# Spectral layer on one core: an inverse transform from quarter-length even waves, one pool of shared buffers, stores from another queue

## The chip, the core and the metric

The kernel runs on one NeuronCore of a Trainium2 chip (trn2). Its engines are TensorE (PE in the profile, its weight loads PEld), VectorE (DVE), ScalarE (ACT), GpSimd (POOL) and SyncE (SP), which only issues transfers. A transfer (DMA) can be issued from the queue of SyncE, ScalarE or GpSimd; an issue waits in its queue behind everything ahead of it. The metric is the device time of one execution in microseconds; the time given for a kernel is the median of its runs. All arithmetic is in float32; a float32 matmul shows as two records in the profile.

## The reference, cut to what matters

The input has shape (4, 512, 128, 64): batch, time, node n, channel c. Layer 0 (a recurrent mixing, two convolutions and a feed-forward part, with layer norms) takes most of the time and the change doesn't touch it. Layer 1 is:

```python
def layer1(x, w_real, w_imag):                 # x: (B=4, T=512, N=128, C=64)
    trend = moving_average(x, 25)              # over time, edges repeated
    seasonal = x - trend
    xs = rfft(seasonal, axis=1)[:, :128]       # the first 128 modes
    ys = einsum('bmnc,cmk->bknc', xs, w_real + 1j * w_imag)   # mixes modes, per channel
    filt = irfft(pad(ys), n=512, axis=1)       # modes above 127 are zero
    return trend + filt
```

## The kernel before

Layer 0 leaves its result in four arrays of HBM, `x4[b]`, each 512 times by 8192 columns (node and channel). Layer 1 (`layer1` in the source) works on them in slabs of 512 columns: 16 slabs per batch, each loaded as a tile `xin` of 128 partitions by 4 blocks of 128 times by 512 columns, 1024 KB, from SyncE's queue (`slab`, L763). It handles the batches in two pairs, and each pair goes through three stages.

*Transform* (32 slabs of a pair). VectorE forms sums and differences of the two halves of the time axis (L780, tiles `uv`). TensorE multiplies the sums with the waves of the even modes and the differences with those of the odd modes (L791), into PSUM banks of the tag `a`, on top of a correction for the edges of the moving average (L787), whose 12 first and 12 last times come from GpSimd's queue as four small transfers per slab (`edge`, L775 and L776, two buffers). ScalarE copies the result into the spectrum `xf` (L796), which holds two planes, real and imaginary, for both batches of the pair. The modes lie in an order of their own on the partitions, `MODES`: before, the 64 even ones and then the 64 odd ones.

*Mix*. In 16 groups of four channels, the weights are loaded (`w`, L803, 512 KB from SyncE's queue, two buffers); GpSimd writes their negated imaginary part beside them (L804); TensorE multiplies spectrum and weights (L811, L815) into banks of the tag `b`, and VectorE and ScalarE copy back into `xf`.

*Inverse* (`invert`, 16 slabs for each batch of the pair). `waves(s)` makes the filtered signal of slab `s`. For each of the two quarters `i` of the first half of the time axis it multiplies real and imaginary plane, even modes (partitions 0 to 63) and odd modes (64 to 127) apart, so eight matmuls with 64 rows (L840), into four banks `a`. ScalarE copies the even part out (L845), and VectorE forms even plus odd, the signal of the quarter, and even minus odd, that of the same quarter of the second half (L848, tiles `pm`). `trends(s)` loads the slab once more, and six small pieces of 12 times each (`halo`, L859 and L862, SyncE's queue, two buffers), computes the moving average of each of the four blocks (L865, and L868 for what reaches over from the neighbouring blocks) into four banks `b`, adds the filtered signal in place (L871), and stores the slab (L872, from ScalarE's queue).

The slabs of transform and inverse share three buffers. The order of TensorE's work is the order of the source (`manual_schedule`): waves 0, waves 1, trends 0, waves 2, trends 1 and so on, so that the last two `trends` of a batch have no waves between them. For the other engines a scheduler fixes the order of the instructions when the kernel is built; each queue then works strictly in that order, and a tile is reused when everything that reads it is done.

Of the kernel before, what the change touches and what calls it, by code (L numbers as in the profile page):

```python
# [10 lines left out]
F32 = mybir.dt.float32  # L11
AF = mybir.ActivationFunctionType
ALU = mybir.AluOpType
# [3 lines left out]
P = 128  # L17
# [14 lines left out]

MODES = np.concatenate([np.arange(0, M, 2), np.arange(1, M, 2)])
EPS = 1e-5
# [5 lines left out]
@with_exitstack  # L40
def conv_seq_kernel(
    ctx: ExitStack,
    tc: tile.TileContext,
    x: bass.AP,
    xt: bass.AP,
    vecs: bass.AP,
    wkvr: bass.AP,
    wo: bass.AP,
    wdec: bass.AP,
    wconv: bass.AP,  # L50
    fbias: bass.AP,
    w1: bass.AP,
    fb1: bass.AP,
    w2: bass.AP,
    fb2: bass.AP,
    wri: bass.AP,
    dft: bass.AP,
    dfte: bass.AP,
    idft: bass.AP,
    avg: bass.AP,  # L60
    avgh: bass.AP,
    out: bass.AP,
):
    B = x.shape[0]
    dram = ctx.enter_context(tc.tile_pool(name="dram", bufs=1, space=DRAM))
    x4 = [dram.tile([T, D], F32, tag=f"x4_{b}", name=f"x4_{b}") for b in range(B)]

    layer0(tc, dram, x, xt, vecs, wkvr, wo, wdec, wconv, fbias, w1, fb1, w2, fb2, x4)
    layer1(tc, x4, wri, dft, dfte, idft, avg, avgh, out)

# [648 lines left out]
@with_exitstack  # L719
def layer1(ctx, tc, x4, wri, dft, dfte, idft, avg, avgh, out):  # L720

# [18 lines left out]
    dfte_sb = load("dfte_sb", dfte)  # L740
    idft_sb = load("idft_sb", idft)
    avg_sb = load("avg_sb", avg)
    avgh_sb = load("avgh_sb", avgh)

    def bank(tag):
        return ps.tile([P, SL], F32, tag=tag, name=tag)
# [14 lines left out]
    def slab(b, s):  # L761
        xin = io.tile([P, NT, SL], F32, tag="xin", name="xin", bufs=3)
        nc.sync.dma_start(  # L763
            xin, x4[b][:, s * SL : (s + 1) * SL].rearrange("(c p) d -> p c d", p=P)
        )
        return xin

    def transform(b, xf):

        for s in range(NS):  # L770
            c = slice(s * SL, (s + 1) * SL)
            xin = slab(b, s)
            edge = io.tile([H, SL], F32, tag="edge", name="edge")
            for r in range(2):
# [23 lines left out]
    def mix(xf):  # L798

        xc = xf.rearrange("p b r (a c l) -> p b r a c l", c=H, l=2)  # L800
        for g in range(H // CG):
            w = io.tile([P, CG, 3, M], F32, tag="w", name="w")
            nc.sync.dma_start(w[:, :, 0:2, :], wri[:, g * CG : (g + 1) * CG, :, :])  # L803
            nc.gpsimd.tensor_scalar(w[:, :, 2, :], w[:, :, 1, :], -1.0, 0.0, ALU.mult, ALU.add)  # L804
            for q in range(CG // 2):
                c0 = g * CG + 2 * q
                py = [bank("b"), bank("b")]
                for r in range(2):
                    for j in range(2):
                        o = py[r][:, j * G * NF : (j + 1) * G * NF]  # L810
                        nc.tensor.matmul(  # L811
                            o, lhsT=w[:, 2 * q + j, r, :], rhs=xc[:, :, 0, :, c0 + j, :], start=True,
                            stop=False,
                        )
                        nc.tensor.matmul(  # L815
                            o, lhsT=w[:, 2 * q + j, 2 if r == 0 else 0, :], rhs=xc[:, :, 1, :, c0 + j, :],
                            start=False, stop=True,
# [9 lines left out]
    def invert(b, xf):  # L827
# [3 lines left out]
        def waves(s):  # L831

            c = slice(s * SL, (s + 1) * SL)
            out = []
            for i in range(2):
                eo = [bank("a"), bank("a")]
                for r in range(2):
                    for h in range(2):
                        hs = slice(h * H, (h + 1) * H)
                        nc.tensor.matmul(  # L840
                            eo[h], lhsT=idft_sb[hs, r, i, :], rhs=xf[hs, r, c],
                            start=(r == 0), stop=(r == 1),
                        )
                even = io.tile([P, SL], F32, tag="even", name="even")
                nc.scalar.copy(even, eo[0])  # L845
                pm = io.tile([P, 2, SL], F32, tag=f"uv{i}", name="pm")
                for k, op in enumerate((ALU.add, ALU.subtract)):
                    nc.vector.tensor_tensor(pm[:, k, :], even, eo[1], op)  # L848
                out.append(pm)
            halves[s] = out  # L850

        def trends(s):
            c = slice(s * SL, (s + 1) * SL)
            xin = slab(b, s)
            halo = io.tile([P, SL], F32, tag="halo", name="halo")
            for j in range(NT):
# [13 lines left out]
            for j in range(NT):  # L870
                nc.vector.tensor_tensor(by_n(xin[:, j, :]), by_n(po[j]), by_c(pm[j % 2][:, j // 2, :]), ALU.add)  # L871
            nc.scalar.dma_start(out[b, :, c].rearrange("(c p) d -> p c d", p=P), xin)  # L872

# [16 lines left out]
def _constants():  # L890
# [20 lines left out]
    idft = waves * weight  # L911
    idft[1, k == 0] = 0.0
    tiles = [slice(i * P, (i + 1) * P) for i in range(NT)]
    avg = np.stack([a[s, s].T for s in tiles], axis=1)
    avgh = np.zeros((NT, 32, P))
    for j, s in enumerate(tiles):
# [5 lines left out]
        "dfte": dfte.reshape(2 * 32, M),  # L922
        "idft": idft[:, :, : T // 2].reshape(2, M, 2, P).transpose(1, 0, 2, 3),
        "avg": avg,
# [5 lines left out]
def _inputs(x, i):  # L930
# [13 lines left out]
    for a in range(2):  # L944
        for b in range(2):
            wconv[a * H : (a + 1) * H, b * H : (b + 1) * H] = taps[a - b + 1]
    wconv[H:, 2 * H :] = taps[0]
    wconv[:H, 2 * H :] = taps[2]
    b = x.shape[0]
    a = {  # L950
# [11 lines left out]
        "fb2": np.concatenate([i["ffn_b2"]] * 2)[:, None],  # L962
        "wri": np.stack([i["w_real"], i["w_imag"]], axis=2)[:, MODES][..., MODES].transpose(1, 0, 2, 3),
        **_constants(),
# [19 lines left out]
```

## Time and profile before

The time is 4107.79 us (median of 3 runs, 4098.11 to 4113.56); the profiled run has a span of 4116.7 us. Layer 1 takes about the last 1130 us of it:

| stage | from to (us) | length | PE busy | DVE busy | ACT busy | DMA GB/s |
|---|---|---|---|---|---|---|
| transform, first pair | 2988 to 3147 | 159 | 158.1 | 73.8 | 39.9 | 249 |
| mix | 3147 to 3259 | 112 | 111.8 | 26.8 | 23.7 | 71 |
| inverse | 3259 to 3553 | 294 | 275.8 | 159.5 | 36.6 | 235 |
| transform, second pair | 3553 to 3706 | 153 | 153.0 | 75.7 | 39.9 | 262 |
| mix | 3706 to 3817 | 111 | 110.8 | 26.4 | 23.7 | 67 |
| inverse | 3817 to 4108 | 291 | 273.2 | 157.5 | 36.6 | 232 |

How to read a group of instructions in the profile: source line, engine and operation; what is written and read by the program's names; shapes; number of instructions; after the bar the time in which at least one of them ran and the mean nanoseconds of one; after the second bar the idle time of the engine just ahead of them, and what ended most of it. Matmuls overlap, so the mean of one is longer than the distance from one start to the next; the prediction works with distances. In a timeline a row is a start, a length and the instructions that were merged into it, with the wait ahead of it in brackets.

### The profile page before, as it was taken

The numbers are of one execution on the slowest core, as the hardware profiler recorded it, in microseconds if no ns is written. First come the engines' busy times: TensorE is split into PE (matmuls) and PEld (weight loads), VectorE is DVE, ScalarE is ACT, GpSimd is POOL, SyncE is SP. The second block draws the span as 40 slices with busy tenths as digits, with TensorE's granted clock in tenths as the row PEclk, the third lists the DMA queues.
The fourth block names the chain that finished last, engine by engine and source line by source line (L and its number), as shares of the span: only waits on it lengthen the run. The fifth ranks groups of instructions, "written<-read, shape, count | busy, mean of one in ns | idle before, by whom it ended". The sixth has DMA issues, their size and how long they took to land. (4 is left out here: it accounts for less than half of the span.)

```text
span 4116.7 us, 46561 instructions
## 1 busy us (share of the span) xinstructions
PE 3908.1 (95%) x16939; PEld 1460.7 (35%) x16939; DVE 2493.7 (61%) x3168; ACT 1796.8 (44%) x2396; POOL 527.2 (13%) x942
## 2 busy tenths in 40 slices
PE   9999989999999999999999888999899999999998
PEld 4433322233333223333322322333325733228433
DVE  1145549975556997555699899655443355542555
ACT  2112336545555554555565678777622211122111
POOL 0000012310000221000122122000032000130000
PEclk9989999999999999999999999999999999999999
DMA  5466647776664776666477676555385377882577
GB/s 170 157 209 235 208 132 250 252 246 228 238 224 152 240 258 237 222 234 231 157 249 250 217 251 238 187 168 184 133 254 168 95 258 243 272 245 72 186 241 239
DMA packets 445854, 867.80 MB, mean 211 GB/s; under 512 B 35321, under 2 KB 101561, under 8 KB 445625
## 3 DMA queue, kind: packets, MB, share of 16 engines
q1 hardware_dynamic: 347136, 588.34, 44.6%
q0 software_dynamic: 62464, 207.66, 14.4%
q10 hardware_dynamic: 36024, 68.82, 4.5%
q8 instruction: 135, 2.21, 0.2%
q14 instruction: 95, 0.77, 0.1%
HBM read 596.18 MB, written 268.50 MB: 210 GB/s over the span
## 5 line engine op out<-in xcount | busy, mean ns | idle before, releaser
L616 PE MATMUL pa<-mid,w_sb 128*64 128x512 f32 x2048 | 499.7, 609 | 43.0 <-DVE x4t L621 42.6
L609 ACT ACTIVATE mid<-m,fb_sb 128x1024 f32<-128x1024 f32 x256 | 285.0, 1113 | 303.4 <-PE m L605 303.0
L621 DVE SCALAR_TENSOR_TENSOR x4t<-pa,fb_sb,x 128x512 f32<-128x512 f32 x252 | 188.0, 746 | 263.2 <-PE pa L616 263.2
L605 PE MATMUL m<-x,w_sb 64*128 64x512 f32 x1008 | 290.8, 650 | 5.7 <-ACT mid L609 5.2
L555 DVE SCALAR_TENSOR_TENSOR to<-xh,vec,to 128x512 f32<-128x512 f32 x384 | 277.0, 744 | 12.6 <-issue 8.6
L609 ACT ACTIVATE mid<-c,fb_sb 128x1024 f32<-128x1024 f32 x256 | 283.3, 1107 | 1.4 <-PE c L605 1.2
L845 ACT COPY even<-a 128x512 f32<-128x512 f32 x128 | 71.7, 588 | 480.3 <-PE b L865 145.8
L865 PE MATMUL b<-xin,avg_sb 128*128 128x512 f32 x512 | 246.6, 626 | 35.5 <-DMA xin<-x 32.4
L605 PE MATMUL c<-x,w_sb 64*128 64x512 f32 x1008 | 264.5, 598 | 0.7 <-ACT mid L609 0.7
L616 PEld LDWEIGHTS pa<-mid,w_sb 128*64 128x64 f32 x2048 | 124.8, 136 | 387.7 <-issue 229.8
L780 DVE TENSOR_TENSOR uv<-xin 128x1024 f32<-128x1024 f32 x128 | 151.2, 1222 | 172.4 <-PE a L791 135.7
L327 PE MATMUL a<-xp,both 128*128 128x512 f32 x512 | 247.5, 610 | 6.4 <-DVE both L324 5.9
L848 DVE TENSOR_TENSOR pm<-even,a 128x512 f32<-128x512 f32 x256 | 159.3, 683 | 143.5 <-ACT even L845 109.7
L791 PE MATMUL a<-uv,dft_sb 128*64 128x512 f32 x1024 | 241.2, 612 | 0.0
L840 PE MATMUL a<-xf,idft_sb 64*128 64x512 f32 x1024 | 239.8, 602 | 0.6 <-DVE pm L848 0.4
L871 DVE TENSOR_TENSOR xin<-b,pm 128x512 f32<-128x512 f32 x256 | 159.1, 684 | 116.4 <-PE b L868 116.4
L634 ACT COPY ob<-pt 128x512 f32<-128x512 f32 x256 | 148.9, 582 | 165.5 <-PE pt L630 165.2
L324 DVE TENSOR_SCALAR both<-both,vec 128x192 f32<-128x192 f32 x192 | 53.2, 316 | 251.9 <-DMA both<-in_wkvr 220.6
L796 ACT COPY xf<-a 128x512 f32<-128x512 f32 x128 | 80.9, 632 | 266.1 <-PE a L791 266.1
L215 PE MATMUL st<-x,ones 128*32 128x512 f32 x512 | 182.4, 615 | 14.3 <-DVE x L491 14.3
L582 ACT ACTIVATE kd<-kd,vec 128x512 f32<-128x512 f32 x256 | 193.5, 809 | 4.3 <-DVE kd L574 4.2
L494 ACT ACTIVATE sq<-x 128x1024 f32<-128x1024 f32 x128 | 134.6, 1052 | 117.7 <-DVE x L491 117.4
(234 smaller groups left out, 6879.3 us busy)
## 6 DMA issues: line engine op xcount, KB each, us to landing
xp<-in_xt SPq DMA_DIRECT2D x256, 512.0 KB
xin<-x SPq DMA_DIRECT2D x128, 1024.0 KB
kx<-x SPq DMA_DIRECT2D x224, 512.0 KB
x<-x POOLq DMA_DIRECT2D x128, 512.0 KB, 4.2
kh<-to SPq DMA_DIRECT2D x128, 512.0 KB
x<-ob POOLq DMA_DIRECT2D x64, 1024.0 KB, 6.6
out<-xin ACTq DMA_DIRECT2D x64, 1024.0 KB
both<-in_x SPq DMA_DIRECT2D x96, 512.0 KB
```

Of the source, the lines that this page charges most:

```text
L215: nc.tensor.matmul(st[32 * q : 32 * q + 32, :], lhsT=ones, rhs=src[:, j, :], start=first, stop=last,)
L327: nc.tensor.matmul(pa[:, k, :], lhsT=wq[:, j, k * P : (k + 1) * P], rhs=xp[:, j, :], start=first and j == 0, stop=last and j == 1,)
L555: nc.vector.scalar_tensor_tensor(to[:, j, :], xh[:, j, k : SL + k], vec[:, w, c], to[:, j, :], ALU.mult, ALU.add)
L582: tc.keep_in_program_order(nc.scalar.activation(d[:, j, :], d[:, j, :], AF.Identity, bias=vec[:, B4, c], scale=vec[:, G4, c]))
L605: nc.tensor.matmul(pm[:, h, :], lhsT=w1_sb[hs, m * P : (m + 1) * P], rhs=x3[hs, :], start=True, stop=True)
L609: nc.scalar.activation(mid, pm, AF.Gelu_apprx_tanh, bias=fb1_sb[:, m : m + 1])
L616: nc.tensor.matmul(pa[h * H : (h + 1) * H, :], lhsT=w2_sb[:, m, :], rhs=mid[:, h, :], start=(m == 0), stop=(m == 1),)
L621: nc.vector.scalar_tensor_tensor(x4t, pa, fb2_sb, x3s[c // 2][:, c % 2, :], ALU.add, ALU.add)
L791: nc.tensor.matmul(pf[r][h * H : (h + 1) * H, :], lhsT=dft_sb[:, h, i, r, :], rhs=uv[h][:, i, :], start=False, stop=(i == 1),)
L840: nc.tensor.matmul(eo[h], lhsT=idft_sb[hs, r, i, :], rhs=xf[hs, r, c], start=(r == 0), stop=(r == 1),)
L848: nc.vector.tensor_tensor(pm[:, k, :], even, eo[1], op)
L865: nc.tensor.matmul(po[j], lhsT=avg_sb[:, j, :], rhs=xin[:, j, :], start=True, stop=False)
```

## The change

The even modes are split by parity once more, which halves the work on them: multiples of 4 are the same in the first and second quarter of the time axis, and the modes 2, 6, 10 and so on change sign. So one matmul each over a quarter of the axis is enough for them, and VectorE forms sum and difference (`even`) before it adds and subtracts the odd part (`pm`) as before. For this the spectrum is laid out anew by the mix: plane 0 holds the even modes, real and imaginary parts of the multiples of 4 on partitions 0 to 63 and those of the others on 64 to 127, and plane 1 all odd modes, real parts and imaginary parts. A matmul of the inverse thus sums over real and imaginary part at once. The weights come from the host in this layout, and GpSimd makes their second plane in four operations (swapped parts, with a sign on one of them).

Further: slabs and weights share one pool of five buffers of 8 KB per partition, instead of three for slabs and two for weights; `halo` and `edge` share two; and the finished slab is stored from GpSimd's queue instead of ScalarE's. The matrices `idft` are replaced by `idfte` (128 by 128) and `idfto` (128 by 2 by 128).

```diff
-MODES = np.concatenate([np.arange(0, M, 2), np.arange(1, M, 2)])
+MODES = np.concatenate([np.arange(0, M, 4), np.arange(2, M, 4), np.arange(1, M, 2)])
...
-        xin = io.tile([P, NT, SL], F32, tag="xin", name="xin", bufs=3)
+        xin = io.tile([P, NT, SL], F32, tag="big", name="xin", bufs=5)
...
-            edge = io.tile([H, SL], F32, tag="edge", name="edge")
+            edge = io.tile([P, SL], F32, tag="edge", name="edge")
...
-            w = io.tile([P, CG, 3, M], F32, tag="w", name="w")
-            nc.sync.dma_start(w[:, :, 0:2, :], wri[:, g * CG : (g + 1) * CG, :, :])
-            nc.gpsimd.tensor_scalar(w[:, :, 2, :], w[:, :, 1, :], -1.0, 0.0, ALU.mult, ALU.add)
+            w = io.tile([P, CG, 2, 2, M], F32, tag="big", name="w", bufs=5)
+            nc.sync.dma_start(w[:, :, 0, :, :], wri[:, g * CG : (g + 1) * CG, :, :])
+            for r, n in ((0, 2), (1, 1)):
+                wr, wi = (w[:, :, k, r, :].rearrange("p c (n i m) -> p c n i m", n=n, i=2) for k in range(2))
+                for i, sign in ((0, -1.0), (1, 1.0)):
+                    if n == 1:
+                        src, dst = wr[:, :, 0, 1 - i, :], wi[:, :, 0, i, :]
+                    else:
+                        src, dst = wr[:, :, :, 1 - i, :], wi[:, :, :, i, :]
+                    nc.gpsimd.tensor_scalar(dst, src, sign, 0.0, ALU.mult, ALU.add)
...
-            out = []
+            ev, od = [bank("a"), bank("a")], [bank("a"), bank("a")]
+            for h in range(2):
+                hs = slice(h * H, (h + 1) * H)
+                nc.tensor.matmul(ev[h], lhsT=idfte_sb[hs, :], rhs=xf[hs, 0, c], start=True, stop=True)
             for i in range(2):
-                eo = [bank("a"), bank("a")]
-                for r in range(2):
-                    for h in range(2):
-                        hs = slice(h * H, (h + 1) * H)
-                        nc.tensor.matmul(
-                            eo[h], lhsT=idft_sb[hs, r, i, :], rhs=xf[hs, r, c],
-                            start=(r == 0), stop=(r == 1),
-                        )
-                even = io.tile([P, SL], F32, tag="even", name="even")
-                nc.scalar.copy(even, eo[0])
+                nc.tensor.matmul(od[i], lhsT=idfto_sb[:, i, :], rhs=xf[:, 1, c], start=True, stop=True)
+            even = io.tile([P, 2, SL], F32, tag="ev", name="even")
+            two = io.tile([P, SL], F32, tag="even", name="two")
+            nc.scalar.copy(two, ev[1])
+            halves[s] = []
+            for i, op in enumerate((ALU.add, ALU.subtract)):
+                nc.vector.tensor_tensor(even[:, i, :], ev[0], two, op)
+            for i in range(2):
                 pm = io.tile([P, 2, SL], F32, tag=f"uv{i}", name="pm")
                 for k, op in enumerate((ALU.add, ALU.subtract)):
-                    nc.vector.tensor_tensor(pm[:, k, :], even, eo[1], op)
-                out.append(pm)
-            halves[s] = out
+                    nc.vector.tensor_tensor(pm[:, k, :], even[:, i, :], od[i], op)
+                halves[s].append(pm)
...
-            halo = io.tile([P, SL], F32, tag="halo", name="halo")
+            halo = io.tile([P, SL], F32, tag="edge", name="halo")
...
-            nc.scalar.dma_start(out[b, :, c].rearrange("(c p) d -> p c d", p=P), xin)
+            nc.gpsimd.dma_start(out[b, :, c].rearrange("(c p) d -> p c d", p=P), xin)
```

## The prediction

> **What bounds the kernel now.** I read the page first (busy shares, slices, costliest groups), then a table of stages, then the timeline of a few slabs, then who waited for whom.
>
> ```profile
> PE 3908.1 (95%) x16939; PEld 1460.7 (35%) x16939; DVE 2493.7 (61%) x3168; ACT 1796.8 (44%) x2396; POOL 527.2 (13%) x942
> L845 ACT COPY even<-a 128x512 f32<-128x512 f32 x128 | 71.7, 588 | 480.3 <-PE b L865 145.8
> L865 PE MATMUL b<-xin,avg_sb 128*128 128x512 f32 x512 | 246.6, 626 | 35.5 <-DMA xin<-x 32.4
> L848 DVE TENSOR_TENSOR pm<-even,a 128x512 f32<-128x512 f32 x256 | 159.3, 683 | 143.5 <-ACT even L845 109.7
> L840 PE MATMUL a<-xf,idft_sb 64*128 64x512 f32 x1024 | 239.8, 602 | 0.6 <-DVE pm L848 0.4
> ```
>
> TensorE is busy 95% of the time, and the matmuls that the diff rewrites (L840) occupy 239.8 us. They hardly wait (0.6 us). The averaging matmuls behind them (L865) do: 32.4 us for the slab, xin. So the edit can pay in two places, array time and waits. The two inverse stages, with the columns span, busy us of PE, PEld, DVE, ACT, POOL, clock, DMA share, GB/s:
>
> ```profile
> 3259.00:3553.00 294.00, 275.80 (x1026) 105.77 (x1026) 159.54 (x255) 36.59 (x66) 0.62 (x1) 0.97 0.73 235
> 3817.00:4108.00 291.00, 273.15 (x1023) 105.64 (x1025) 157.51 (x254) 36.59 (x66) 0.00 (x0) 0.98 0.71 232
> ```
>
> Together 585 us for 64 slabs. An undisturbed slab in the timeline (start, length, engine):
>
> ```profile
> 3423.14 3.70 PE L840 MATMUL a<-xf,idft_sb 64*128 64x512 f32 x16
> 3425.74 0.38 ACTq L872 DMA_DIRECT2D out<-xin  x1
> 3426.22 1.29 ACT L845 COPY even<-a 128x512 f32<-128x512 f32 x2 [7.04 <-DVE xin L871]
> 3426.77 3.70 PE L865 MATMUL b<-xin,avg_sb 128*128 128x512 f32 x8
> 3426.84 2.48 DVE L848 TENSOR_TENSOR pm<-even,a 128x512 f32<-128x512 f32 x4 [1.13 <-PE a L840]
> 3430.40 1.14 PE L868 MATMUL b<-halo,avgh_sb 12*128 12x512 f32 x8
> 3430.91 0.38 SPq L763 DMA_DIRECT2D xin<-x  x1
> 3431.47 3.70 PE L840 MATMUL a<-xf,idft_sb 64*128 64x512 f32 x16
> ```
>
> From start to start: waves 3.63, averages 3.63, halo 1.07, one slab 8.33 us, no gap on PE. 64 x 8.33 = 533 us; the remaining 52 us of the 585 are stalls. The next fence shows the end of a batch, where the averages of the last two slabs follow each other:
>
> ```profile
> 3386.39 0.38 SPq L763 DMA_DIRECT2D xin<-x  x1
> 3386.42 0.45 ACTq L872 DMA_DIRECT2D out<-xin  x1
> 3394.40 6.03 PE L865 MATMUL b<-xin,avg_sb 128*128 128x512 f32 x8 [3.75 <-DMA xin<-x]
> 3395.20 0.38 SPq L763 DMA_DIRECT2D xin<-x  x1
> ```
>
> A slab load leaves only when the store of three slabs earlier has landed (xin has 3 buffers): 5.2 us after its issue in the quiet case (3425.74 to 3430.91), 8.8 us when a load and a store leave together (3386.42 to 3395.20). The load then takes 8.0 us (3386.39 to 3394.40). Ring: adds 2.5 + store 8.8 + load 8.0 = 19.3 us, plus issue and semaphore steps, against 3 x 8.33 - 4.70 = 20.3 us from a slab's halo matmuls to the averages three slabs later. The ring just closes, and any delay reaches PE. Comparing each start-to-start time with the undisturbed one, over all 64 slabs: 18 us between waves and averages, 17 us before and 14 us within the last averages of the four batches, 4 us at their first two waves.
>
> **What the Trainium skill says.** "TensorE: Matmul & The Clock Gate", Part 3: matmuls in different row groups run concurrently. The trace agrees: 16 records of 64 rows (L840) take the 3.63 us of 8 records of 128 rows (L865). "TensorEngine Tiling (Array Packing)", Key Properties: changing the tiling mode drains TensorE. The trace fits: records within a run start 0.427 us apart (weight loads at 3428.16, 3428.59, 3429.02), 8 x 0.427 = 3.42, so a change of form costs 0.21. "DMA: Bandwidth & Descriptors", Issuing engines are not separate DMA queues: a store issued from another engine gains no bandwidth. The queue table agrees: 44.6% for 588 MB, 14.4% for 208 MB and 4.5% for 69 MB are all 0.065 to 0.076% per MB. The tensor engine page's specifications: ScalarE, VectorE and GpSimd queues are strict first in, first out; the even copy above starts only after ACT has issued the store, 0.5 us behind it.
>
> **The change, part by part.**
>
> *Inverse matmuls.* Per slab 8 matmuls (16 records, 8 pair-times) become one concurrent pair with 64 rows (2 pair-times) and two matmuls with 128 rows (4 record-times): 6 x 0.427 = 2.56 instead of 3.42. Form changes per slab stay three: halo to pair, pair to full, averages to halo; full to averages is now none. Waves 3.63 becomes 2.78, a slab 7.48. Gain 0.85 x 64 = 54.6 us, all on PE, which has no gap to hide it in.
>
> *VectorE and ScalarE.* Per slab two more tensor_tensor: 6 for the waves and 4 for the adds, each 0.62 (2.48 / 4): 6.2 us inside 7.48. In order: adds from 0.1 to 2.6 us after the halo matmuls, the six to 6.3, all before the next adds at 7.6. PSUM banks come free before PE asks: the first even bank at 3.9, od at 6.3, needed at 7.5. ScalarE loses one copy of 0.59 and all stores. Nothing on the path.
>
> *Five buffers shared by slabs and weights.* The ring becomes 5 x 7.48 - 4.70 = 32.7 us for the same 19 to 20 us, so the slab is no longer what PE waits for. What replaces it: the halo loads. In the changed order of SyncE's queue halo s+3 stands behind slab load s+5, which waits for store s. From halo matmuls s to s+3 there are 3 x 7.48 = 22.4 us for adds 2.6, store, load 8.0 and about 1 for the small transfers that follow: 18.2 us with a store of 6.6, 21.2 with 9.6 (below). It closes, with 1 to 4 us to spare.
>
> *Stores from GpSimd.* Not shown before in this stage; the nearest row is the 1024 KB store of the first layer from the same queue, 4.6/6.6/9.6 us (lowest, median, highest) from issue to landing, 0.75 us on GpSimd. I take the median. ScalarE's copy no longer queues behind the store. Behind the stores on GpSimd now stand the edge loads of the next pair of batches: the last load of edge 1 waits for the last adds, 2.6 + 0.75 + 0.5 + 4.0 (edge, issue to landing) = 7.9 us after the last halo matmuls, where one slab of the transform lasts 4.6 us. About 4 us once, with edge 0.
>
> *Weights.* One GpSimd operation of 0.62 us per group of four channels becomes four of half the size, 1.2 to 2.5 us; a group lasts 6.9 us (8 x 2 records x 2 at 0.217), and GpSimd waited 216 us there. Hidden, but edges 13 to 15 of each second batch now stand behind weight groups 0 to 2, whose loads wait for a shared buffer: I find some 1.5 us too late, 0 to 3 per pass, so 3 us. The spectrum's start (15.3 us wait for the first edge) is untouched, as is layer 0.
>
> *Stalls left.* First two waves of a batch 1.0 and 1.65 (twice each), 5.3; the last averages waiting for the adds' banks 0.8 x 4 = 3.2; the edges 4. That is 12.5 of the 54 us; with 10 us for slabs where transfers bunch (bounds 0 and 30) 22.5. Gain 31.
>
> *Sum.* -54.6 - 31 + 3 (edges behind weights) + 1 (last store from GpSimd) = -81.6: 4107.8 - 81.6 = 4026 us.
>
> **DMA.** A slab moves 2.10 MB and six halo pieces of 24 KB, 2.24 MB. At 7.48 us that is 300 GB/s, at a measured share of about 0.73 for 235 GB/s a share of 0.93. This is the unknown. Best: a 10 us window inside the first inverse stage (3340 to 3350) shows 329 GB/s, 6.8 us per slab. Middle: the bunched store took 3.6 us longer than the quiet one for about 1.05 MB more, 290 GB/s, 7.7 us. Worst: the bunched pair, 2.24 MB in 8.0 us, 280 GB/s, latency included. I take PE's 7.48 and let the 10 us above stand for the middle case (64 x 0.2 = 13).
>
> **The rivals.**
> - *DMA becomes the bound.* For it: the 0.93. Against: the 8.0 us contain latency that more buffers overlap. At 8.0 us a slab 64 x 8.0 + 12.5 = 524 against 585, -61, and +4: 4051 us.
> - *Only the matmuls pay*, since waits move from slab to halo or store: -54.6 + 4 = 4057 us. For it: 22.4 against 18 to 21 us.
> - *Everything hides better than feared*: no bunching, edges in time: -54.6 - 43 = 4010 us.
> - *Slower.* The halo ring does not close: adds 2.6, store 9.6, load 8.4, six issues 2.4 and landing 4.0 one after another, 27 us per three slabs, 9.0 each: 576 + 12.5, and edges late by 3 us in 16 slabs: about +10 to +15, 4120 us. Against: the six issues overlap the load.
>
> **How the numbers follow.** Forecast 0.52, DMA bound 0.20, matmuls only 0.12, better 0.10, slower 0.06 (within it a part that ends at no change). The range reaches from just below the better case, 4004, to just over the two middling rivals, 4064. 0.5% is 20.5 us: faster 0.92, same 0.04, slower 0.04.
>
> **What would show it.** Waves 2.78 us from start to start and a period near 7.5; L865 without "DMA xin"; no halo wait before the halo matmuls; DMA near 300 GB/s in the inverse. Wrong would be: a period of 8 with DMA waits (bound by transfers), gaps before the halo matmuls (the new ring), gaps before the edge matmuls in slabs 13 to 15 or in the first two of the second pass, or waves over 3 us (a cost of the change of form that I have not seen).

## The result, and the profile after

The changed kernel takes 4011.5 us (median of 4 runs, 4003.66 to 4020.01), the kernel before, beside it on the same chip, 4110.68 us (4 runs, 4098.11 to 4119.38): ratio 0.9764 [0.9735, 0.9792], 99 us less. The forecast was 4026.

Below, gains are (1 - ratio) x 4110 us, because a ratio takes out what differs from chip to chip; that makes 97 us for the change. First the engines and two of the costliest groups of the page of after (columns as before):

```profile
PE 3836.3 (95%) x16427; PEld 1426.3 (35%) x16427; DVE 2564.5 (64%) x3296; ACT 1762.6 (44%) x2332; POOL 605.4 (15%) x1102
L877 PE MATMUL b<-xin,avg_sb 128*128 128x512 f32 x512 | 230.8, 593 | 3.3 <-DVE xin L883 3.3
L854 ACT COPY two<-a 128x512 f32<-128x512 f32 x64 | 37.5, 586 | 428.8 <-PE a L849 428.8
```

PE's busy time falls by 72 us and keeps its share of 95%. The averages, which waited 35.5 us before, wait 3.3 us, and none of it for a slab. ScalarE's copy now waits for TensorE alone. The two inverse stages, in the columns of the same table of before:

```profile
3243.00:3490.00 247.00, 243.75 (x769) 92.23 (x768) 195.72 (x322) 19.51 (x34) 25.59 (x35) 1.00 0.84 277
3764.00:4008.00 244.00, 241.14 (x760) 90.65 (x756) 192.08 (x316) 19.05 (x33) 23.50 (x31) 0.99 0.81 268
```

The span falls from 294 to 247, and the part of it in which PE is idle from 18 to 3 us. An undisturbed slab of after in the timeline:

```profile
3336.24 1.13 PE L849 MATMUL a<-xf,idfte_sb 64*128 64x512 f32 x4
3336.33 2.49 DVE L883 TENSOR_TENSOR xin<-b,pm 128x512 f32<-128x512 f32 x4 [1.41 <-PE b L880]
3337.30 1.98 PE L851 MATMUL a<-xf,idfto_sb 128*128 128x512 f32 x4
3339.11 0.75 POOL L884 DMA_DIRECT2D out<-xin  x1 [6.72 <-DMA halo<-x]
3339.12 3.60 PE L877 MATMUL b<-xin,avg_sb 128*128 128x512 f32 x8
3342.65 1.14 PE L880 MATMUL b<-halo,avgh_sb 12*128 12x512 f32 x8
3343.72 1.13 PE L849 MATMUL a<-xf,idfte_sb 64*128 64x512 f32 x4
```

From start to start the waves take 1.06 + 1.82 = 2.88 us, the averages 3.53, the halo matmuls 1.07: one slab 7.48 us. Layer 1 by stages, from the first matmul of one stage to that of the next in the two traces (the last stage up to the start of its last matmul):

| stage | before | after |
|---|---|---|
| transform 1 | 159.2 | 150.3 |
| inverse 1 | 294.0 | 247.3 |
| transform 2 | 152.9 | 161.3 |
| inverse 2 | 290.6 | 245.4 |
| mixes, both | 223.4 | 223.4 |

The inverse gained 584.6 - 492.7 = 92 us: 64 x (8.33 - 7.48) = 54 of array time, and 37 of stalls (51 before, 14 after). Of the 37 us, 30 are idle time of PE (36 to 6 in the two tables of stretches); the rest goes with the granted clock, 0.97 and 0.98 before, 1.00 and 0.99 after. The transforms together differ by 0.5 us: 9 us gained in the first and 8 lost in the second. The 9 us are no clear gain of the change, for over the profiles of this study, one for each kernel, the first transform took 150 to 159 us. The remaining 7 us between the two profiles lie ahead of layer 1, which starts at 2988.1 in one and 2981.1 in the other; over the same profiles, all with the same layer 0, that start spreads from 2974 to 2993.

The waits of PE in layer 1 of after (total, times, longest, in us):

```profile
PE a L791 <- DMA edge<-x: 20.4, 3, 15.2
PE b L877 <- DVE xin L883: 3.3, 5, 0.8
PE b L880 <- DMA halo<-x: 2.5, 3, 1.3
```

The wait of 15.2 us is the start of layer 1, as before. The others for `edge` are the new ones, at the change from the first inverse to the second transform and near the end of that transform:

```profile
3495.52 1.97 PE L791 MATMUL a<-edge,dfte_sb 24*64 24x512 f32 x4 [3.95 <-DMA edge<-x]
...
3634.66 1.97 PE L791 MATMUL a<-edge,dfte_sb 24*64 24x512 f32 x4 [1.31 <-DMA edge<-x]
```

Each costs more than its wait. From start to start the first takes 8.0 us more than an undisturbed slab of the transform (4.6 us), the second 5.7 us more. The table of stretches says why; for the first wait they are the slab's edge matmuls with the wait, its other matmuls (L795), and the slabs after it:

```profile
3490.00:3497.00 7.00, 3.05 (x11) 0.51 (x8) 4.21 (x5) 0.00 (x0) 2.79 (x5) 0.59 1.05 402
3497.40:3503.00 5.60, 5.60 (x18) 1.52 (x16) 0.00 (x0) 0.62 (x1) 2.00 (x4) 0.63 1.03 336
3504.00:3510.00 6.00, 6.00 (x34) 1.75 (x32) 3.76 (x4) 1.26 (x2) 2.95 (x6) 1.00 1.05 354
```

The mean clock (third column from the right) is 0.59 and 0.63 in the first two and 1.00 only in the third: 16 records of L795 take 5.6 us in place of 3.6. In the trace's clock records the clock is at half from 3491.3 to 3501.6, and after the second wait from 3634.7 to 3641.5. It is the same in the kernel before, where the averages of the prediction's second fence take 6.03 us after a wait of 3.75. The Trainium skill, "TensorE: Matmul & The Clock Gate", Part 1, describes this: the clock is gated by how busy TensorE has been of late, over windows of about 3.4 us. The trace agrees on the windows: 10.2 and 6.8 us are three and two times 3.4. It does not fit a full idle window as the condition, for the second gap lasted 1.31 us. Nor does every such gap lower the clock: in the trace of before, gaps of 1.40 and 1.81 us (at 3522 and 3485) were followed by none.

So in the main it looks as forecast. Whether it came about as forecast is another question: the sum credits the stall gain to the five buffers and nothing to the queue of the store.

### The profile page after: what moved, and what is told of

Same layout as the page of the kernel before. It is cut to its first block, busy times and chain, and to the rows that moved or that the text cites. A ratio compares the mean times of both kernels' runs of the same rounds, so it can differ in the third digit from the quotient of the medians.

```text
span 4018.2 us, 45619 instructions
## 1 busy us (share of the span) xinstructions
PE 3836.3 (95%) x16427; PEld 1426.3 (35%) x16427; DVE 2564.5 (64%) x3296; ACT 1762.6 (44%) x2332; POOL 605.4 (15%) x1102
## 5 line engine op out<-in xcount | busy, mean ns | idle before, releaser
L606 PE MATMUL m<-x,w_sb 64*128 64x512 f32 x1008 | 290.6, 649 | 5.8 <-ACT mid L610 5.2
L328 PE MATMUL a<-xp,both 128*128 128x512 f32 x512 | 243.8, 603 | 6.4 <-DVE both L325 5.9
L795 PE MATMUL a<-uv,dft_sb 128*64 128x512 f32 x1024 | 239.6, 611 | 0.0
L877 PE MATMUL b<-xin,avg_sb 128*128 128x512 f32 x512 | 230.8, 593 | 3.3 <-DVE xin L883 3.3
L854 ACT COPY two<-a 128x512 f32<-128x512 f32 x64 | 37.5, 586 | 428.8 <-PE a L849 428.8
L883 DVE TENSOR_TENSOR xin<-b,pm 128x512 f32<-128x512 f32 x256 | 159.2, 684 | 100.2 <-PE b L880 85.3
L325 DVE TENSOR_SCALAR both<-both,vec 128x192 f32<-128x192 f32 x192 | 53.2, 316 | 247.3 <-DMA both<-in_wkvr 208.8
L637 POOL DMA_DIRECT2D x<-ob x64 | 49.0, 766 | 1057.5 <-ACT ob L635 988.1
L322 DVE BATCH_NORM_STATS2 stt<-both 128x6 f32<-128x512 f32 x192 | 124.4, 685 | 94.7 <-DMA both<-in_x 93.6
```

The lines of the kernel that those rows point to most:

```text
L328: nc.tensor.matmul(pa[:, k, :], lhsT=wq[:, j, k * P : (k + 1) * P], rhs=xp[:, j, :], start=first and j == 0, stop=last and j == 1,)
L606: nc.tensor.matmul(pm[:, h, :], lhsT=w1_sb[hs, m * P : (m + 1) * P], rhs=x3[hs, :], start=True, stop=True)
L795: nc.tensor.matmul(pf[r][h * H : (h + 1) * H, :], lhsT=dft_sb[:, h, i, r, :], rhs=uv[h][:, i, :], start=False, stop=(i == 1),)
L877: nc.tensor.matmul(po[j], lhsT=avg_sb[:, j, :], rhs=xin[:, j, :], start=True, stop=False)
```

## The experiments

Three parts can be had alone: the new *waves*, the shared *buffers*, and the *store* on GpSimd's queue. An edit is shown against after or before, as said. Times are medians of 4 to 20 runs, ratios are against the kernel before, run beside each on the same chip. In the row of a list of waits stand the total, the times and the longest, in us.

**The waves alone** (after, with the buffers and the store of before):

```diff
-        xin = io.tile([P, NT, SL], F32, tag="big", name="xin", bufs=5)
+        xin = io.tile([P, NT, SL], F32, tag="xin", name="xin", bufs=3)
...
-            w = io.tile([P, CG, 2, 2, M], F32, tag="big", name="w", bufs=5)
+            w = io.tile([P, CG, 2, 2, M], F32, tag="w", name="w", bufs=2)
...
-            nc.gpsimd.dma_start(out[b, :, c].rearrange("(c p) d -> p c d", p=P), xin)
+            nc.scalar.dma_start(out[b, :, c].rearrange("(c p) d -> p c d", p=P), xin)
```

> The changed kernel with three buffers for slabs and two for weights again, and the store from ScalarE's queue again: of the change only the new waves (and the layout they need) is left. Ring theory (slab load waits for the store three slabs earlier, the ring costs adds 2.5 + store 8 to 8.8 + load 8 + averages and halo 4.6, some 24 to 25 us for three slabs, so 8.0 to 8.3 us a slab whatever TensorE needs): most of the 54.6 us of array time turns into waits for xin, 4085 to 4105 us, waits of the averages for xin above 50 us. Additive theory (array time and waits are separate gains): 54.6 us come off, 4055 us, waits for xin as before, about 32 us.

4101.78 us, ratio 0.998 [0.997, 0.999]: 8 us of the 54 that the waves take off the array. The array time is gone, but a wait has taken its place:

```profile
PE b L877 <- DMA xin<-x: 62.7, 40, 4.0
```

**The buffers alone** (before, `xin` and `w` from one tag of five buffers):

```diff
-        xin = io.tile([P, NT, SL], F32, tag="xin", name="xin", bufs=3)
+        xin = io.tile([P, NT, SL], F32, tag="big", name="xin", bufs=5)
...
-            w = io.tile([P, CG, 3, M], F32, tag="w", name="w")
+            w = io.tile([P, CG, 3, M], F32, tag="big", name="w", bufs=5)
```

> The kernel before with slabs and weights in five shared buffers, all else as before. Both theories: the stalls of 50 us in the inverse shrink to about 13, 64 slabs at 8.33 us, about 4072 us (4065 to 4082). If the gain of the buffers came from elsewhere (for instance the stores' queue), there would be no gain: 4100 us or more.

4092.81 us, ratio 0.9954 [0.9939, 0.997]: 19 us, half of what the stalls gave in the change, and between the two forecasts. The wait for the slab is gone from the list of waits, yet stalls stay: the two inverse stages take 289.4 and 282.5 us, 572 in place of 585. The largest wait of PE in them is now for ScalarE's copy, and next to it stand 7.6 us for VectorE's adds:

```profile
PE a L840 <- ACT even L845: 8.1, 2, 4.1
```

**The edge loads from ScalarE's queue** (after, L779 and L780):

```diff
-                nc.gpsimd.dma_start(edge[32 * r : 32 * r + HALO, :], x4[b][0:HALO, c])
-                nc.gpsimd.dma_start(edge[32 * r + HALO : 32 * r + 2 * HALO, :], x4[b][T - HALO : T, c])
+                nc.scalar.dma_start(edge[32 * r : 32 * r + HALO, :], x4[b][0:HALO, c])
+                nc.scalar.dma_start(edge[32 * r + HALO : 32 * r + 2 * HALO, :], x4[b][T - HALO : T, c])
```

> The changed kernel with the edge loads of the transform issued from ScalarE's queue, away from the stores and the weights' operations on GpSimd. My theory: the late edges at the start of the second transform (6.0 and 2.0 us) and behind the weights at its end (3.3 and 2.4 us) vanish, 3997 to 4005 us. Rival: the edges now stand behind ScalarE's copies of the spectrum and come late in many slabs, 4011 to 4030 us.

4014.21 us, ratio 0.9765 [0.9742, 0.9789], no difference from after. The late edges at the weights are gone, but others are late at the start of both transforms (from start to start 3.6 and 2.0 us lost in the first; 4.1, 2.5, 1.9 and 2.7 in the second); transform 2 takes 158.8 us in place of 161.3. Another queue alone does not help. Whether GpSimd's queue made them late in after, this run can't say, since it trades one lateness for another; the run with more buffers below does.

**The change without the new store** (after, the store from ScalarE's queue):

```diff
-            nc.gpsimd.dma_start(out[b, :, c].rearrange("(c p) d -> p c d", p=P), xin)
+            nc.scalar.dma_start(out[b, :, c].rearrange("(c p) d -> p c d", p=P), xin)
```

> The changed kernel with the finished slab stored from ScalarE's queue again. My theory: the copy of the second even bank moves behind the store, to about 3.0 us into a slab, the six operations of VectorE then end just before the next adds, nothing reaches TensorE: within 6 us of the changed kernel, 4005 to 4018 us. Rival (the move of the store is part of the gain, since VectorE has little slack): the period grows by 0.1 to 0.5 us, 4018 to 4045 us.

4077.75 us, ratio 0.9915 [0.9893, 0.9937]. One line, costed at no gain, is worth 97 - 35 = 62 us, more than either theory had. Its timeline tells why; "SPq" and "ACTq" are transfers issued by SyncE and ScalarE:

```profile
3331.60 2.47 DVE L883 TENSOR_TENSOR xin<-b,pm 128x512 f32<-128x512 f32 x4
...
3335.50 0.38 SPq L767 DMA_DIRECT2D xin<-x  x1
3335.53 0.45 ACTq L884 DMA_DIRECT2D out<-xin  x1
...
3336.07 0.59 ACT L854 COPY two<-a 128x512 f32<-128x512 f32 x1 [8.10 <-PE b L877]
...
3336.69 1.29 DVE L857 TENSOR_TENSOR even<-a,two 128x512 f32<-128x512 f32 x2 [2.62 <-ACT two L854]
...
3344.31 0.38 SPq L767 DMA_DIRECT2D xin<-x  x1
3344.33 0.45 ACTq L884 DMA_DIRECT2D out<-xin  x1
```

The adds end at 3334.08, but the store leaves at 3335.53, 30 ns after the next load. The same pair leaves together again 8.8 us later. Something releases both at once. ScalarE's copy, behind the store in its queue, is late with it, VectorE waits 2.62 us for the copy, and TensorE's banks come free late.

The waits that each issue carries, which the trace records, name it. Every transfer issued by SyncE or ScalarE signals one of eight completion semaphores (100 to 107 in the trace), given out in turn over both queues; GpSimd's transfers have eight of their own (111 to 118). An issue waits until the transfer that had its semaphore before has landed, the one eight transfers earlier. With the store on ScalarE there are exactly eight such transfers per slab: one load, six halo pieces, one store. The reason for such a wait is in the Trainium skill, "DMA: Bandwidth & Descriptors", Why a DMA increments its semaphore by 16 and not by 1: two transfers in flight on one semaphore can fill each other's count, so there should be one semaphore for each in flight (no run here shows what happens without the wait). So each load waits for the load before to land, and each store for the store before: one load and one store in flight, however many buffers there are.

The landings in the trace say which of these waits ends last. The load before had landed at 3334.75, the store before at 3335.43; load and store left 0.07 and 0.10 us after the latter. For the store this is the turn. For the load it is its buffer: of five, it takes the one whose slab has just been stored. SyncE's own waits, from 3250 to 3480, have the same two:

```profile
SPq L767 <- DMA out<-xin: 130.4, 24, 6.6
SPq L767 <- DMA xin<-x: 3.6, 1, 3.6
```

One landing thus releases both, they travel together, and the store takes some 8.7 us again. It is not so in every slab. In the second inverse stage of the same kernel there is a run of eight slabs in which the load leaves 1 to 3 us after the store, as soon as the load before has landed. There the stores leave on time, land after some 5 us, and follow each other at 7.2 to 7.5 us. The columns are those of the table of stretches, the first row from that run, the second from a stretch in step:

```profile
3861.00:3921.00 60.00, 57.64 (x184) 21.56 (x182) 45.86 (x76) 4.10 (x7) 0.00 (x0) 1.00 0.93 307
3280.00:3340.00 60.00, 59.10 (x166) 20.75 (x164) 40.27 (x67) 4.10 (x7) 0.00 (x0) 1.00 0.77 248
```

Moving the store to GpSimd leaves seven per slab on the shared eight, and one on GpSimd's. This is the theory that the following runs test; I call it the turn theory. The rivals are ScalarE's queue (the copy behind the store, wherever the store's wait comes from) and the buffers.

**Nine transfers per slab in place of eight** (the kernel with ScalarE's store, one halo piece split in two):

```diff
-                    nc.sync.dma_start(halo[at : at + HALO, :], x4[b][(j + 1) * P : (j + 1) * P + HALO, c])
+                    if j == 0:
+                        nc.sync.dma_start(halo[at : at + 6, :], x4[b][P : P + 6, c])
+                        nc.sync.dma_start(halo[at + 6 : at + HALO, :], x4[b][P + 6 : P + HALO, c])
+                    else:
+                        nc.sync.dma_start(halo[at : at + HALO, :], x4[b][(j + 1) * P : (j + 1) * P + HALO, c])
```

> The changed kernel with the store from ScalarE's queue, and the first halo piece of each slab loaded as two pieces of six times, so that SyncE and ScalarE issue nine transfers per slab instead of eight. Turn theory: the transfers of these two queues take their completion semaphores in turn from eight, and an issue waits until the transfer eight places earlier has landed; with eight per slab a store waits for the store before it and a load for the load before it; with nine both wait for small pieces long landed. So the store leaves right after the adds, and most of the 66 us that the ScalarE store cost come back: 4010 to 4028 us, store issues about 0.1 us after the adds. Queue theory (the copy of the even bank stands behind a store that waits for the adds): nothing changes, 4065 to 4085 us.

4069.14 us, ratio 0.9895 [0.9877, 0.9913]: it did not free the store, and the turn theory's forecast of 4010 to 4028 us failed. The largest wait of its ScalarE in the inverse stage:

```profile
ACT two L854 <- DMA halo<-x: 90.7, 11, 10.2
```

The store's predecessor is now a halo piece, as intended, but that piece stands behind a load of 1 MB in SyncE's queue and lands as late as a store would: of the 36 stores of this trace that leave over 0.5 us late, 34 leave 0.07 to 0.10 us after the landing of the piece that had their semaphore before. So the time agrees with the turn theory only after the fact, and does not separate it from the queue theory; the landings are as the turn has it.

**The store alone** (before, the store from GpSimd's queue; the edit is the last line of the change's diff):

> The kernel before with only the store moved to GpSimd's queue; old waves, three slab buffers. Turn theory: seven transfers per slab are left on the two queues, so neither stores nor loads wait for the one before; adds 2.5, issue 0.8, store 6.6, load 7, averages and halo 4.7 are 21.6 us against three slabs of 8.33, most of the 18 us between waves and averages and part of the 31 us at the batches' ends go: 4070 to 4090 us. Ring theory of the prediction (landing times alone, three buffers): no gain, 4103 to 4116 us.

4079.89 us, ratio 0.9923 [0.9905, 0.9941]: 32 us, with three buffers and the old waves. Of the parts alone this is the most.

**Waves and store** (the first experiment, with the store on GpSimd; three buffers):

> The changed kernel with three slab and two weight buffers again, store on GpSimd as changed. Turn theory with three buffers: the ring of 23 to 24 us over three slabs gives 7.7 to 8.0 us per slab against 7.48 of array time, 4030 to 4060 us with waits for xin. If the number of buffers hardly matters once the store has left the shared turn: 4008 to 4020 us.

4055.84 us, ratio 0.9867 [0.9852, 0.9882]: 55 us. Here the ring of three buffers, as the prediction described it, shows undisturbed: the slab still makes PE wait, 23.2 us in place of 62.7, and the waits for edges in layer 1 come to 27.0 us with the 15.0 of its start. Of the 42 us between this kernel and the change, 14 lie in the two transforms (325.3 and 311.6 us in the two profiles).

```profile
PE b L877 <- DMA xin<-x: 23.2, 17, 4.2
```

**Buffers and store** (before, with both):

> The kernel before (old waves) with five shared buffers and the store from GpSimd: the change without its new waves. Array time 64 x 8.33 = 533 us and the 10 to 13 us of stalls that the changed kernel has left in its inverse stages: 545 against 585, some 4 us back for late edges, 4070 to 4076 us, hence 58 to 65 us for the waves once buffers and store have changed. If the waves' gain is limited to array time and nothing else moves, changed minus this is 54.6 us, within 6.

4062.02 us, ratio 0.9884 [0.9869, 0.9899]: 48 us, more than expected; inverse stages 269.6 and 268.6 us, where 32 x 8.33 = 267 would be a stage without stalls. All stalls but 2 to 3 us per stage are gone without the waves.

**The halo loads from GpSimd, the store from ScalarE** (after; the two halo loads and the store change queue):

```diff
-                    nc.sync.dma_start(halo[at : at + HALO, :], x4[b][j * P - HALO : j * P, c])
+                    nc.gpsimd.dma_start(halo[at : at + HALO, :], x4[b][j * P - HALO : j * P, c])
...
-                    nc.sync.dma_start(halo[at : at + HALO, :], x4[b][(j + 1) * P : (j + 1) * P + HALO, c])
+                    nc.gpsimd.dma_start(halo[at : at + HALO, :], x4[b][(j + 1) * P : (j + 1) * P + HALO, c])
...
-            nc.gpsimd.dma_start(out[b, :, c].rearrange("(c p) d -> p c d", p=P), xin)
+            nc.scalar.dma_start(out[b, :, c].rearrange("(c p) d -> p c d", p=P), xin)
```

> The changed kernel with the store from ScalarE's queue and instead the six halo pieces from GpSimd's queue. SyncE and ScalarE then issue two transfers per slab, so the transfer eight places earlier in their common turn is four slabs old. Turn theory: stores leave within 0.1 us of the adds, as the GpSimd stores do (0.3 us), and the 66 us come back nearly whole: 4010 to 4030 us. Queue theory (what costs is that ScalarE's copy of the even bank stands behind the store, whenever that leaves): 4055 us or more.

4005.2 us, ratio 0.9748 [0.9728, 0.9769]. The store is back on ScalarE ahead of the copy, and all 62 us stay: the store need not be on GpSimd's queue. On the shared eight are two transfers per slab, so a store's predecessor is four slabs old. In the timeline:

```profile
3338.48 0.44 ACTq L884 DMA_DIRECT2D out<-xin  x1
...
3339.01 0.59 ACT L854 COPY two<-a 128x512 f32<-128x512 f32 x1 [6.95 <-PE a L851]
...
3343.44 2.48 DVE L883 TENSOR_TENSOR xin<-b,pm 128x512 f32<-128x512 f32 x4
...
3345.96 0.44 ACTq L884 DMA_DIRECT2D out<-xin  x1
```

The adds end at 3345.92 and the store leaves 0.04 us later; stores are 7.48 us apart.

**The copy ahead of the store** (the kernel with ScalarE's store; the store of a slab is issued after the copy of the next waves, and ScalarE's order is written out too):

```diff
-            nc.gpsimd.dma_start(out[b, :, c].rearrange("(c p) d -> p c d", p=P), xin)
+            done.append((c, xin))
+
+        done = []
+
+        def store():
+            if done:
+                c, xin = done.pop()
+                nc.scalar.dma_start(out[b, :, c].rearrange("(c p) d -> p c d", p=P), xin)
...
                 waves(s)
+            store()
             if s > 0:
                 trends(s - 1)
+        store()
...
-    with tc.manual_schedule(engines={nc.tensor.engine}):
+    with tc.manual_schedule(engines={nc.tensor.engine, nc.scalar.engine}):
```

> The changed kernel with the store from ScalarE's queue, but issued one slab step later in the program, so that the copy of the next slab's even bank stands ahead of the store and not behind it; eight transfers per slab as in the version with the ScalarE store. Queue theory (the copy behind the held store costs the time): 4010 to 4030 us. Turn theory in its strong form (stores follow one another's landing, at 8.6 to 8.8 us, and loads likewise, so transfers set the pace even with the copy free): 4050 to 4075 us, stores 8.5 us or more apart.

4079.97 us, ratio 0.9926 [0.9912, 0.9941], as slow as with the copy behind the store. So the held store costs as much without the copy behind it: the pair of load and store sets the pace by itself. What reaches TensorE here are the halo pieces, which stand behind the held load in SyncE's queue (17.3 us of waits, 11 times). The issues of the pair are still 8.7 us apart and still together:

```profile
3334.53 0.38 SPq L767 DMA_DIRECT2D xin<-x  x1
3334.54 0.45 ACTq L891 DMA_DIRECT2D out<-xin  x1
...
3343.26 0.38 SPq L767 DMA_DIRECT2D xin<-x  x1
3343.27 0.45 ACTq L891 DMA_DIRECT2D out<-xin  x1
```

Over all kernels, a store's lateness (from the end of the last add to the issue, over the 64 stores of a trace) sorts them into two kinds:

| kernel | transfers per slab on the shared eight | mean lateness, us | late by over 0.5 us | median distance of stores, us |
|---|---|---|---|---|
| before | 8 | 1.14 | 34 | 8.80 |
| waves alone | 8 | 1.23 | 44 | 8.88 |
| buffers alone | 8 | 1.57 | 37 | 8.76 |
| change, store on ScalarE | 8 | 1.08 | 39 | 8.77 |
| the same, copy first | 8 | 3.57 | 47 | 8.74 |
| nine transfers | 9 | 0.99 | 36 | 8.59 |
| store alone | 7 | 0.33 | 2 | 8.34 |
| buffers and store | 7 | 0.33 | 2 | 8.34 |
| waves and store | 7 | 0.33 | 2 | 7.48 |
| after | 7 | 0.33 | 2 | 7.48 |
| halo on GpSimd | 2 | 0.03 | 0 | 7.48 |

In the rows of eight and nine the transfers set the period of most slabs, 8.6 to 8.9 us whether a slab is 7.48 or 8.33 us of matmuls; in those of seven and two the matmuls do. In the five rows of eight, 201 stores are late; 197 of them leave 0.07 to 0.10 us after the landing of the transfer that had their semaphore before, and in 180 of these that was the store before. With the store on ScalarE, at least the first three stores of a stage, with none in flight ahead of them, are only 0.03 us late.

**More buffers for edges and halos** (after; to make room, one buffer for `ev`):

```diff
-            edge = io.tile([P, SL], F32, tag="edge", name="edge")
+            edge = io.tile([P, SL], F32, tag="edge", name="edge", bufs=4)
...
-            even = io.tile([P, 2, SL], F32, tag="ev", name="even")
+            even = io.tile([P, 2, SL], F32, tag="ev", name="even", bufs=1)
...
-            halo = io.tile([P, SL], F32, tag="edge", name="halo")
+            halo = io.tile([P, SL], F32, tag="edge", name="halo", bufs=4)
```

> The changed kernel with four buffers for edge and halo instead of two, paid for with one buffer instead of two for the sum and difference of the even banks (written and read by VectorE alone, in order). If late edges at both ends of the second transform and at the end of the first come from the two buffers: 8 to 13 us come off, 3998 to 4004 us, and the waits for edge after the first shrink from 5 us to under 1. If they come from the order on GpSimd (edges behind stores and behind the weights' operations): within 4 us of the changed kernel, 4008 to 4016 us.

3999.25 us, ratio 0.9727 [0.9711, 0.9744], 12 us below after, though the two intervals just touch. The change had put `edge` and `halo`, with two buffers each before, into two shared ones. With four, and GpSimd's queue as it was, only the start of layer 1 still waits for an edge, and no halo is late:

```profile
PE a L791 <- DMA edge<-x: 14.7, 1, 14.7
```

Transform 2 takes 148.1 us (161.3 in after), the inverse stages 243.1 and 242.1 (247.3 and 245.4): layer 1, from its first matmul to the end, 1018.3 in place of 1037.1 us.

**Both** (halos on GpSimd, store on ScalarE, and the four buffers):

> The changed kernel with the store from ScalarE's queue, the halo pieces from GpSimd's, four buffers for edge and halo and one for the sum and difference of the even banks. If the two gains are separate (6 us for a store that leaves 0.3 us earlier and no edges behind stores, 12 us for edge buffers): 3988 to 3996 us. If they remove the same late edges: 3996 to 4004 us, level with the four-buffer version.

4004.85 us, ratio 0.974 [0.9727, 0.9754]: no further gain. Layer 1 takes 1016.5 us, level with 1018.3. In the profiles it starts 9 us later than with the four buffers alone (2992.7, 2983.6), within the spread of that start, so the medians can't rank the two. The halos on GpSimd without the four buffers had inverse stages of 243.8 and 243.3 us and a second transform of 152.6; the four buffers alone give as much or more in each of these three, which fits that there was little left to add.

## Why the prediction was right, and where it was not

- **Inverse matmuls: right, the last digit by luck.** A slab is 7.48 us, as worked out. Within it the waves are 2.88 us and not 2.78, and the averages 3.53 and not 3.63: I gave the passage from full to averages no cost, and it has about 0.1 us; the averages up to the halo take 0.1 us less than before. The two errors cancel.
- **VectorE and ScalarE: right.** VectorE waits 1.41 us for the halo matmuls in the slab shown, which fits 7.48 - 6.2 = 1.3.
- **"A slab load leaves only when the store of three slabs earlier has landed": incomplete.** It is true, and with the waves, three buffers and the store on GpSimd it costs 23 us of waits. But with eight transfers per slab a store also waits for the store before it, which needs no buffer, and the sum of the ring left this hold out. In the prediction's second fence the adds ended at 3384.28 (their row stands below) and the store left at 3386.42: with these 2.1 us the ring is 21.4 us against 20.3, and does not close. I took 8.8 us for a load and a store that leave together as the latency of a bad moment; it was the period of the transfers. Before, stores were 8.80 us apart with 8.33 us of matmuls: a part of the kernel was already bound by this.
- **"Stores from GpSimd", no gain and a small cost: this step failed.** The 62 us of the change that go with it are the largest error of the prediction. The argument that an issue from another engine gains no bandwidth does not answer the question, because the held issues were waiting for a landing, and not for bandwidth: the DMA engines moved 246 GB/s in the first inverse stage with the store on ScalarE, and 277 in after. Its costs were right in kind and too small: the edges at the change of passes cost 8.0 us where I had 4, since I counted the wait (3.95 us) and not the slow clock after it; the last store from GpSimd costs 0.9 (7.9 to 8.8 us from the last matmul to the end), where I had 1.
- **"Five buffers", credited with the stall gain: failed as an attribution.** Alone they give 19 us. The stall gain of 37 us (31 predicted) needs both store and buffers.
- **Stalls left: near.** 14 us remain in the inverse stages. The sum had 8.5 there, 4 for the edges, and 10 for the bunching of transfers. It took them from 54 us of stalls, where its own figures give 52 (585 - 533) or 53 (18 + 17 + 14 + 4). The distance from 4026 to 4011.5 is 14.5 us: layer 1 gained 1128.6 - 1037.1 = 91.5 us in the two profiles where the sum had 81.6, and the rest lies ahead of layer 1.
- **Weights and edges behind them: right in place, half in size.** Edges are late near the end of transform 2 and not of transform 1; a wait of 1.3 us costs 5.7 with the slow clock, where I had 3 us over both passes. The two places cost 13.7 us together, and more buffers give 13.2 of them back.
- **DMA as the bound (0.20): no.** At 7.48 us a slab the first inverse stage moves 277 GB/s, DMA share 0.84, and PE waits for no slab. *Only the matmuls pay* (4057) and *slower*: no. The sum of *slower* does not give its figure: 576 + 12.5 is 3.5 us over the 585, and 3 us in 16 slabs would be 48 more, where the two together were to be 10 to 15. *Everything hides better* (4010) gave nearly the measured number; its premise, no bunching, held, its other one, edges in time, held only with more buffers.

The total came out by luck, because the error of attribution lay within one sum: buffers and store were made together, and the sum needed only what both bring. On the parts it would have been wrong each time: waves alone 8 us and not 54, buffers alone 19 and not 31 to 43, store 62 on top of the others and not 0.

The waits of before held the hint, and I passed over it. In its first inverse stage, ScalarE's even copy waits, in total, times, longest:

```profile
ACT even L845 <- DMA out<-xin: 64.3, 7, 16.5
```

A copy that reads PSUM waits for no store; what waited was the store ahead of it in the queue, and a store that waits for a store has no buffer to wait for. The timeline had it too: the row of the adds that end 2.1 us ahead of the store of 3386.42 is

```profile
3381.79 2.49 DVE L871 TENSOR_TENSOR xin<-b,pm 128x512 f32<-128x512 f32 x4 [1.38 <-PE b L868]
```

Alone, the three parts give 8 + 19 + 32 = 59 us; together 97. On top of the other two, waves are worth 49 (97 - 48), buffers 42 (97 - 55), the store 62 (97 - 35). Each of the three bounds the period of a slab: where the pair of transfers takes 8.8 us, faster matmuls have nothing to gain.

*Left open*: why a load and a store that leave together move 248 GB/s and out of step 307, and what brings them in and out of step. And no run changed the number of semaphores: the turn theory rests on the waits and landings of the traces, the table of lateness, and the two ways of leaving the eight.

## What to carry to other kernels

Count the transfers that one round of a loop issues on queues that share a set of completion semaphores: when the count meets the size of the set, each transfer waits for its own twin of the round before, and more buffers don't lift that wait (on top of the waves they gave 27 us with it, 35 - 8, and 42 without it). Read what the small engine waits for, too: "copy waits for store" is a queue, and its cause stands one instruction ahead. And where several waits bound the same period, measure the parts together and one by one, since the sum of the parts (59 us here) says little about the whole (97).

## What was unexpected of the hardware

- A mixed load and store of 1 MB each, with halos, ran at 277 GB/s over 247 us with TensorE idle for 3 us of them; the same pair, released together, recurs every 8.6 to 8.9 us at 248 GB/s, and out of step in the same kernel every 7.2 to 7.5 us at 307 GB/s.
- After gaps of 3.95 and 1.31 us TensorE's granted clock was at half for 10.2 and 6.8 us, which made the two waits for edges cost 8.0 and 5.7 us.
- Issuing the 1 MB store takes 0.75 us on GpSimd and 0.38 to 0.46 us on ScalarE; it also leaves 0.3 us after the adds and not 0.03.
- GpSimd takes 1.52 us for four operations of 256 elements per partition (L816), 0.37 us from start to start, where one of 512 took 0.62 us before: halving the size saves 40% of an operation and not half.
